# RWKV layers of a four-layer sequence on Trainium2: outer mixes and decays moved beside a unit's spreading, one inner mix interleaved with the decay product, gates held back

## The chip, the core and the metric

The program runs on one core of one Trainium2 chip. The time is the device time of one execution in microseconds; before the change it is 3452.1 us, the median of three runs (3450.18 to 3452.9). One further execution was recorded by the hardware profiler.

Names of engines in the profile: PE is the matrix engine (PEld its weight loads), DVE the vector engine, ACT the scalar engine, POOL the general one, SP the one that mostly issues DMAs (SPq and ACTq are the queues from which DMAs are issued). Each engine runs its own instructions in program order and waits for others through semaphores.

## The reference, cut to what matters

Four layers follow each other: a grouped cross attention, an RWKV block, a second cross attention with a feed-forward part, and another RWKV block. The input x is 16 x 100 x 512. Only the two RWKV blocks (layers 1 and 3) are touched. One of them computes, per batch:

```python
xa = _ln(x, ln1_w, ln1_b)
sx = concat([state[:, 1:2] - xa[:, :1], xa[:, :-1] - xa[:, 1:]], axis=1)
xxx = tanh((xa + sx * maa_x) @ maa_w1).reshape(b, l, 5, 32)
xxx = einsum('blfd,fde->blfe', xxx, maa_w2)
xm = xa[:, :, None] + sx[:, :, None] * (maa_stack + xxx)
xk, xw, xv, xr, xg = (xm[:, :, j] for j in range(5))
w = exp(-exp(time_decay + tanh(xw @ td_w1) @ td_w2))
r, k, v = xr @ Wr.T, xk @ Wk.T, xv @ Wv.T
g = silu(xg @ Wg.T)
# per head, over time: out_t = r_t (u * k_t v_t^T + s);  s = k_t v_t^T + w_t * s
og = groupnorm(out) * gn_w + gn_b
x1 = x + og * g @ Wo.T
# then the channel mix: xk2, xr2 from a second layer norm,
return x1 + sigmoid(xr2 @ Wfr.T) * (square(relu(xk2 @ Wfk.T)) @ Wfv.T)
```

All data are float32. There are 32 heads of 16 channels. The product with `maa_w1` has 160 columns, 32 for each of the five mixes f = 0 (k), 1 (w), 2 (v), 3 (r), 4 (g).

## The kernel before, in words

The 16 batches are taken in NG = 4 groups of G = 4, so a group has T = 400 tokens. The 512 channels lie as NC = 4 chunks of 128 partitions. A product of a chunk with a weight is 128 x 128 by 400 columns, and a full projection of one output chunk is a chain of four such products into one PSUM bank.

**Units.** The recurrence is cut into 128 units per layer: 4 groups x 4 chunks x 8. In one unit u (the loop at the end of `rwkv`):

- `spread(u + 1)`: PE copies rows of v to the 128 partitions, two products of 32 rows each (`vb<-vc,sel`). Even units use rows 0 to 63 of the array, odd ones rows 64 to 127. ACT then puts the starting state in column 0.
- `product(u)` and `scan(u)` on DVE: multiply by k, then two scans over time with w; POOL multiplies the result by r (`a<-a,rr`). There are two `vbs` buffers, so the spreading of unit u + 1 waits for the scan of unit u - 1.
- every second unit `gather`: four products of 32 columns each into the bank `acc` (`acc<-a,gat`); once per chunk (8 units) `bonus` (a product with `ones`, fed by POOL's `rk`, and four with `center`) and `norm` (a product with `mean`, started by `slots.begin()`).

**Pieces.** All other PE work of the layer is cut into pieces, listed by `piece(us, fn, slot, tag)` and taken in order while a budget `due` lasts: each unit adds 2.37 us (u below 29), 2.75, or 3.5 in the last 32 units, minus shares for the gather, bonus and norm, and each piece takes off its listed price. A `chain` is two pieces of two products each. `projections(g, base)` lists a group's pieces and is called at u = 32(g - 1) - 10, so a group's projections run during the units of the group before it; group 0's run ahead of unit 0. In order they are: statistics (DVE), `root` (POOL, gives `rstd` and `shift`) and `normed` (ACT, `xn_a`), priced 0; `turned`: transposes per chunk, ACT writes `ext`, POOL `sx`, then ACT `sm` and POOL `xm`; `inner(0, 128)` and `inner(128, 160)`: the first product with `maa_w1`, whose tanh gives `z0` (mixes 0 to 3) and the upper part of `tz` (mix 4); `mixed(fs, c)`: the second product of a mix for chunk c, 32 rows by 128 columns (mix f lies in rows 32f to 32f + 31; mix 4 in rows 64 to 95), read by DVE (`tm`) one unit later and finished on POOL (`xj`); `plain`: k, v, r; `decay_in`: 128 rows by 64 columns, tanh into the lower part of `tz`; `decay`: 64 rows (0 to 63) by 128 columns, two exponentials on ACT; `gate`: chains with Wg, a tanh on ACT and a product on DVE (`g2`). k, v, r, w and g go to DRAM from ACT's queue and come back through SP's queue.

In the last 32 units the pieces are the channel mix of groups 0 to 2 (`channel_stream`); the output product Wo of a group comes 7 units after its last unit, and group 3's Wo and channel mix follow the last unit.

**Banks.** Three PSUM banks (`Slots`) go round among all pieces. Taking a bank makes the reading of its former content be issued first (`readers`), otherwise `read_later` issues it at `slots.begin()` of the next unit, which stands ahead of the scan on DVE. Instructions of PE, DVE, ACT and POOL keep the program's order; DMAs on SP are placed by the framework.

**Lines.** Nearly all operations are recorded under the lines of helpers (L82 for a product, L85 for a transpose, L77 for DVE, ACT and POOL), so groups are told apart by their tiles: `mm<-z,maa_w2a` is an outer mix 0 to 3, `mm<-tz,td_maa_w` with 32 rows mix 4 and with 64 rows a decay, `mm<-xm,maa_w` the inner mix, `mm<-xj,td_w` the first decay product, `mm<-xj,l_Wg` a gate. The profile counts each float32 product as two MATMUL instructions.

## Time and profile before

| | |
|---|---|
| runs | 3450.18, 3452.1, 3452.9 us |
| the profiled execution | 3447.39 us, span of its instructions 3445.6 us, granted PE clock 0.942 |
| busy over the span | PE 3121.5 us (91%), DVE 1753.5 (51%), POOL 1373.2 (40%), ACT 977.3 (28%) |
| scans, `a<-wr,vb` on DVE | 512 x 971 ns |
| products by k, `vb<-vb,kr` on DVE | 256 x 977 ns |
| products by r, `a<-a,rr` on POOL | 256 x 1880 ns |
| spreadings, `vb<-vc,sel` on PE | 1024 instructions, 252.7 us busy |
| outer mixes 0 to 3 on PE | 256 instructions, 73.6 us busy |
| mix 4 and decays on PE | 128 instructions, 56.5 us busy |
| inner mixes on PE | 128 instructions, 67.4 us busy |

The first unit of layer 1 starts at 845.8 us (its spreading), the last at 1468.6; those of layer 3 at 2733.7 and 3352.6. A row of the windows gives a stretch of the span and the busy time of every engine in it. A row of the timeline gives the start, the time until the last end, engine, line, operation, tiles written and read, and in brackets how long the engine was idle and what ended that. Products overlap in the array: the time between two starts says more than the duration of one, and a product that waits inside the array for its data counts as busy.

### The profile page before, as it was taken

The numbers are of one execution on the slowest core, as the hardware profiler recorded it, in microseconds if no ns is written. First come the engines' busy times: TensorE is split into PE (matmuls) and PEld (weight loads), VectorE is DVE, ScalarE is ACT, GpSimd is POOL, SyncE is SP. The second block draws the span as 40 slices with busy tenths as digits, with TensorE's granted clock in tenths as the row PEclk, the third lists the DMA queues.
The fourth block names the chain that finished last, engine by engine and source line by source line (L and its number), as shares of the span: only waits on it lengthen the run. The fifth ranks groups of instructions, "written<-read, shape, count | busy, mean of one in ns | idle before, by whom it ended". The sixth has DMA issues, their size and how long they took to land. (4 is left out here: it accounts for less than half of the span.)

```text
span 3445.6 us, 47937 instructions
## 1 busy us (share of the span) xinstructions
PE 3121.5 (91%) x18371; PEld 1422.0 (41%) x18371; DVE 1753.5 (51%) x3570; ACT 977.3 (28%) x1715; POOL 1373.2 (40%) x1036
## 2 busy tenths in 40 slices
PE   6989898868999989988999999879998899998997
PEld 3434443334333333334455555445553433333333
DVE  4777777732877766523333333320001287766661
ACT  1333233222233333321323222211111233423332
POOL 0444444443775765521212111220002377676551
PEclk8999999979999989999999999989998999998998
DMA  5010100013335353222000000010011343535321
GB/s 173 22 31 22 31 22 34 1 32 115 113 108 150 109 173 108 77 72 64 28 19 20 19 20 31 26 64 10 10 58 34 111 129 102 150 116 174 91 70 50
DMA packets 171374, 240.18 MB, mean 70 GB/s; under 512 B 27678, under 2 KB 139358, under 8 KB 171146
## 3 DMA queue, kind: packets, MB, share of 16 engines
q1 hardware_dynamic: 148106, 204.35, 19.9%
q10 hardware_dynamic: 23040, 32.78, 2.7%
q8 instruction: 144, 2.36, 0.3%
q14 instruction: 84, 0.69, 0.1%
HBM read 174.25 MB, written 36.04 MB: 61 GB/s over the span
## 5 line engine op out<-in xcount | busy, mean ns | idle before, releaser
L77 POOL TENSOR_TENSOR a<-a,rr 128x800 f32<-128x800 f32 x256 | 480.9, 1880 | 331.0 <-DVE a L77 212.0
L77 DVE TENSOR_TENSOR_SCAN a<-wr,vb 128x400 f32<-128x400 f32 x512 | 475.9, 971 | 20.7 <-PE acc L82 9.1
L77 DVE TENSOR_TENSOR vb<-vb,kr 128x792 f32<-128x792 f32 x256 | 250.1, 977 | 184.7 <-ACT vb L77 184.5
L77 DVE CUSTOM_DVE_ANT_0 junk<-l_sc,mask 100x361 f32<-100x361 f32 x512 | 272.9, 533 | 87.1 <-PE l_sc L82 70.5
L82 PE MATMUL vb<-vc,sel 32*128 32x396 f32 x1024 | 252.7, 565 | 3.3 <-DVE a L77 3.3
L77 DVE TENSOR_TENSOR pt<-l_sc,maskT 121x400 f32<-121x400 f32 x384 | 193.4, 566 | 89.6 <-PE l_sc L82 88.8
L77 ACT ACTIVATE pt<-pt 121x1600 f32<-121x1600 f32 x96 | 147.6, 1538 | 282.4 <-DVE pt L77 280.8
L1490 DVE CUSTOM_DVE_ANT_0 junk<-l2a_sc,mask 100x361 f32<-100x361 f32 x256 | 136.9, 535 | 173.0 <-PE l2a_sc L82 155.8
L1526 POOL TENSOR_TENSOR pa<-pt,pt 121x1600 f32<-121x1600 f32 x16 | 57.1, 3569 | 362.3 <-ACT pt L1521 362.3
L77 POOL TENSOR_TENSOR xj<-tm,ext 128x400 f32<-128x400 f32 x160 | 150.6, 961 | 110.9 <-DVE tm L77 110.1
L77 DVE SCALAR_TENSOR_TENSOR tm<-mm,vec,sx 128x400 f32<-128x400 f32 x160 | 95.7, 628 | 185.5 <-PE mm L82 149.4
L82 PE MATMUL k<-ct,l_k_w 128*128 128x361 f32 x512 | 173.3, 482 | 14.4 <-DMA ct<-in_ctxT 14.4
L1707 DVE TENSOR_TENSOR x<-pb,x 100x512 f32<-100x512 f32 x16 | 12.2, 760 | 335.4 <-DMA pb<-po 330.3
L77 POOL TENSOR_TENSOR pa<-pt,pt 121x1600 f32<-121x1600 f32 x32 | 114.7, 3583 | 165.0 <-ACT pt L77 165.0
L63 PE MATMUL h<-yTb,l_fc 128*128 128x400 f32 x512 | 174.5, 503 | 6.3 <-ACT yTb L229 6.3
L82 PE MATMUL v<-l_v_w,ct 128*121 128x512 f32 x384 | 175.5, 601 | 0.0
L63 PE MATMUL p<-l_proj,h 128*128 128x512 f32 x384 | 165.5, 592 | 0.0
L77 ACT COPY vb<-s0r 128x8 f32<-128x8 f32 x256 | 42.9, 168 | 407.8 <-PE vb L82 320.4
L82 PE MATMUL l_sc<-kz,qz 32*100 32x361 f32 x1024 | 116.7, 526 | 42.9 <-DVE pt L77 22.0
L82 PEld LDWEIGHTS vb<-vc,sel 32*128 32x128 f32 x1024 | 81.9, 191 | 154.0 <-issue 113.5
L63 PEld LDWEIGHTS h<-yTb,l_fc 128*128 128x128 f32 x512 | 97.7, 192 | 81.1 <-ACT yTb L229 8.3
L77 POOL TENSOR_TENSOR pa<-pa,pt 119x1600 f32<-119x1600 f32 x32 | 114.4, 3576 | 41.1 <-ACT pt L77 40.9
(258 smaller groups left out, 5174.2 us busy)
## 6 DMA issues: line engine op xcount, KB each, us to landing
kr<-dk SPq DMA_DIRECT2D x256, 100.0 KB
wr<-dw SPq DMA_DIRECT2D x256, 100.0 KB
rr<-dr SPq DMA_DIRECT2D x256, 100.0 KB
ct<-in_ctxT SPq DMA_DIRECT2D x32, 722.0 KB
dk<-k ACTq DMA_DIRECT2D x32, 200.0 KB
kc<-dk SPq DMA_DIRECT2D x32, 200.0 KB
dw<-wd ACTq DMA_DIRECT2D x32, 200.0 KB
dv<-v ACTq DMA_DIRECT2D x32, 200.0 KB
```

Source lines behind the costliest of these rows:

```text
L63: nc.tensor.matmul(out=ps, lhsT=lhs(c), rhs=rhs(c), start=(c == 0), stop=(c == n - 1))
L77: return lambda *args, **kw: tc.keep_in_program_order(op(*args, **kw))
L82: pin(nc.tensor.matmul(**kw))
L1490: nc.vector.tensor_tensor_reduce(out=junk, in0=ss[r][:L, :S2], in1=t["mask"], scale=-1.0, scalar=FLT_MAX, op0=ALU.add, op1=ALU.min, accum_ ...
L1526: nc.gpsimd.tensor_tensor(t["pa"], t["pt"][0], pt, ALU.add)
L1707: nc.vector.tensor_tensor(x, pb[:, i, :], x, ALU.add)
```

## The change

- `Slots` remembers the bank of an open chain (`held`) and passes it over when a bank is asked for.
- `piece` takes two more values, `half` and `ok`. A new function `beside(u)` is called once per unit, after `slots.begin()` and before `scan(u)`: it takes the first piece whose `half` is u % 2 (row half 0 for mixes 0 and 1 and for the decays, half 1 for mixes 2, 3 and for mix 4), if that piece's `ok` allows it, and charges 0.12 us to the budget. PE gets it right after the spreading of unit u + 1, which uses the other half of the rows, or after the chunk's `mean` product where one is issued at `slots.begin()`.
- `inner` now makes only the first 128 columns. The last 32 (mix 4) are made in `decay_in`: for each chunk one 64-column product with `td_w1` into partitions 0 to 63 of a bank and one 32-column product with `maa_w1` into partitions 64 to 95, and one tanh reads both.
- The order of a group's pieces is new: inner mix, mixes 0 and 1, `decay_in`, all of k, mixes 2 and 3, decays, all of v, all of r, mix 4.
- The gates are not listed with their group but held in `held`: the next group's list takes them in among its first pieces (two half chains ahead of the inner mix, four behind it, two behind `decay_in`), and the last group's stand in the channel stream after its first transposes.
- The budget per unit is 1.9 (from 2.37) for u below 29 and 2.4 (from 2.75) up to the last 32 units.

```diff
         def bank(self):
             t = next(self.turns)
+            if t is self.held:
+                t = next(self.turns)
             self.readers.pop(id(t), lambda: None)()
             return t
...
+            def beside(u):
+                half = u % 2
+                p = next((p for p in pieces if p[4] == half and p[1] <= u), None)
+                if p is None or not p[5]():
+                    return 0.0
+                pieces.remove(p)
+                p[2]()
+                return 0.12
...
+                older, taken = list(pieces), set()
+                behind = [(p[0], base - 1 if g > 1 or i > 3 else -1000, *p[2:]) for i, p in enumerate(held)]
...
                 def decay_in():
+                    bank = []
+                    def half(i):
+                        if i == 0:
+                            for fn in soon + mixes[1]:
+                                fn()
+                            slots.held = slots.bank()
+                            bank.append(slots.held)
+                            begun.append(second)
+                        else:
+                            begun.clear()
+                            slots.held = None
+                        ps = bank[0]
+                        for c in (2 * i, 2 * i + 1):
+                            mm(
+                                out=ps[:64, :T], lhsT=td1[:, c, :], rhs=xj[1][:, c, :],
+                                start=(c == 0), stop=(c == NC - 1),
+                            )
+                            mm(
+                                out=ps[64:96, :T], lhsT=w1[:, c, 128:160], rhs=st["xm"][:, c, :],
+                                start=(c == 0), stop=(c == NC - 1),
+                            )
+                        if i:
+                            scalar.activation(st["tz"], ps[:96, :T], AF.Tanh)
+                            taken.add("tz")
...
-                inner(0, 128)
-                mix((0, 1), 0)
-                mix((0, 1), 1)
-                inner(128, 160)
-                mix((0, 1), 2)
-                mix((0, 1), 3)
+                free = {
+                    (0, 1): lambda: "z0" in taken and not any(p in pieces for p in older),
+                    (2, 3): lambda: "tz" in taken and not any(p in pieces for p in older + behind),
+                    (4,): lambda: "tz" in taken and all(("k", c) in taken for c in range(NC)) and ((2, 3), 0) in taken,
+                }
+                pieces.extend(behind[:2])
+                inner()
+                pieces.extend(behind[2:6])
+                for c in range(NC):
+                    mix((0, 1), c)
+                decay_in()
+                pieces.extend(behind[6:])
                 for c in range(NC):
                     plain(0, "Wk", "k", c)
+                for c in range(NC):
                     mix((2, 3), c)
-                decay_in()
...
+                for co in range(NC):
+                    piece(0.67, lambda co=co: decay(co), late, None, 0, lambda: "tz" in taken)
...
-                for co in range(NC):
-                    gate(co)
+                held[:] = written(lambda: [gate(co) for co in range(NC)])
...
                 for k in ("stats", "normed", "turned"):
                     got += parts[0][k]
+                got += [(p[0], slot - 1, *p[2:]) for p in held]
+                held.clear()
...
                 slots.begin()
+                aside = beside(u) if unit and u + 1 < UNITS else 0.0
                 if unit:
                     scan(u)
...
-                due = min(due, 0.0) + (2.37 if 0 <= u < 29 else 2.75 if u < UNITS - 32 else 3.5 if u < UNITS else 3.9)
+                due = min(due, 0.0) + (1.9 if 0 <= u < 29 else 2.4 if u < UNITS - 32 else 3.5 if u < UNITS else 3.9)
+                due -= aside
```

## The prediction, made before the changed kernel ran

> **What bounds the kernel now.** I read the four 32-unit stretches of the first RWKV layer as a table of windows, then TensorE's timeline inside them, then the other queues at the places where TensorE stood. The windows (start:end, length, then busy us and instructions of PE, PEld, DVE, ACT, POOL, then clock and DMA):
> ```profile
> 845.80:978.70 132.90, 126.09 (x503) 48.95 (x502) 103.26 (x130) 43.51 (x97) 92.38 (x76) 0.93 0.35 107
> 978.70:1128.00 149.30, 143.54 (x578) 55.73 (x576) 109.14 (x137) 49.85 (x105) 99.88 (x82) 0.94 0.43 127
> 1128.00:1293.40 165.40, 151.78 (x587) 57.88 (x586) 111.08 (x139) 55.26 (x113) 113.30 (x97) 0.90 0.48 144
> 1293.40:1468.50 175.10, 162.79 (x713) 64.53 (x712) 107.09 (x133) 64.06 (x127) 95.41 (x77) 0.93 0.31 89
> ```
> PE is the fullest engine in each. Layer 3 repeats them (132.7, 147.5, 166.8 and 172 us), so everything below counts twice. The scan work of DVE is a floor of about 105 us per stretch, POOL's 92 to 113.
>
> What a piece costs on PE, from its timeline:
> ```profile
> 955.32 0.94 PE L82 MATMUL vb<-vc,sel 32*128 32x396 f32 x4
> 956.18 0.88 PE L82 MATMUL acc<-a,gat 128*32 128x400 f32 x8
> 956.99 1.61 PE L82 MATMUL mm<-xj,l_Wg 128*128 128x400 f32 x4
> 958.53 0.60 PE L82 MATMUL vb<-vc,sel 32*128 32x396 f32 x2
> ...
> 1070.16 0.60 PE L82 MATMUL mm<-tz,td_maa_w 32*128 32x400 f32 x1
> 1070.16 0.60 PE L82 MATMUL vb<-vc,sel 32*128 32x396 f32 x2
> 1070.60 0.49 PE L82 MATMUL mm<-tz,td_maa_w 32*128 32x400 f32 x1
> 1070.60 0.50 PE L82 MATMUL vb<-vc,sel 32*128 32x396 f32 x2
> 1071.03 0.88 PE L82 MATMUL acc<-a,gat 128*32 128x400 f32 x8
> ...
> 1203.71 1.61 PE L82 MATMUL mm<-tz,td_maa_w 64*128 64x400 f32 x4
> 1205.24 0.93 PE L82 MATMUL vb<-vc,sel 32*128 32x396 f32 x4
> ```
> Every product is two passes. By starts: a spreading 0.87, a gather 0.81, half a chain (two products) 1.54. Passes of a chain start 0.335 apart, so a product is 0.67 and each change of tile form (rows x columns of the array) costs 1.54 - 2 x 0.67 = 0.20; a lone product is 0.87. The second block is an outer mix beside a spreading, both 32x128, in other rows: together 0.87, so the mix is free. The third is two decays (64x128, rows 0 to 63) ahead of a spreading in rows 64 to 127: free rows too, yet it starts only after the decays' 1.53, 0.43 after their last pass. Same tile form overlaps; another form waits.
>
> Adding these prices over the order of the products gives 117.2, 134.7, 137.4 and 155.1 us for the stretches. Where PE runs through they agree with the clock: units 40 to 47 add to 35.8 and took 35.5, 48 to 55 add to 32.5 and took 32.3. So PE waits 15.7, 14.6, 28.0 and 20.0 us in the stretches (the page counts a product waiting in the array as busy). The waits sit at group starts:
> ```profile
> 823.03 10.91 PE L82 MATMUL mm<-xj,l_Wg 128*128 128x400 f32 x32
> 841.31 0.43 PE L85 MATMUL mm<-ident,xn_a 100*128 100x100 f32 x1 [7.37 <-ACT xn_a L77]
> ...
> 981.42 1.70 PE L82 MATMUL mm<-rk,ones 128*128 128x400 f32 x2 [1.75 <-POOL rk L77]
> 985.85 5.21 PE L82 MATMUL mm<-xm,maa_w 128*128 128x400 f32 x8 [1.23 <-POOL xm L77]
> 990.99 0.93 PE L82 MATMUL vb<-vc,sel 32*128 32x396 f32 x4
> ```
> Ahead of unit 0 PE is out of work after the last gate, because DVE takes group 1's statistics only after that gate's product; POOL's `shift` and ACT's `xn_a` follow. At unit 32 the inner mix takes 5.2 instead of 2.9 us, waiting on POOL's `xm`.
>
> **The change part by part (first layer; all on PE unless said).**
>
> *Mixes beside a spreading.* Of 36 mix pieces in units 0 to 127, 9 already fall next to a spreading in other rows; in the new order 22 do. 13 x 0.87 = -11.3. (Where a chunk's `mean` product is emitted in between, they do not.)
>
> *Decays beside a spreading.* 64x128 after 32x128: no overlap by the 1205.24 row. 12 decays that mostly went in pairs (1.54, so 0.77 each) go alone at 0.87: +1.2. They are charged 0.12 in the budget, so the units carrying them get more work than planned.
>
> *Second inner mix alternating with the first decay product.* No row has a 64-column next to a 32-column product in free columns. Bounds: if columns overlap, eight products take 4 x 0.67 + 0.20 = 2.9 against 6.2 for the four halves before (-3.3 per group); if each alternation waits as rows of unequal height do, 8 x 0.87 = 7.0 (+0.8). I take the second, the nearest row: 3 groups, +2.4. In group 0, ahead of unit 0, the product follows POOL's `xj` (eight at 0.96) anyway, so it is about level there.
>
> [...]
>
> *Budget and pieces cut differently.* A few more half chains and changes of form: +1.2. Together -6.5 on PE. By place, the new order adds to 109.1, 133.0, 132.8 and 153.7 (-15.8) in the stretches, and 9.2 us of channel products that used to lie inside now follow unit 127.
>
> *After unit 127.* Those 9.2 us precede the Wo products; before, PE waited there 4.2 us on POOL's last `gc`, and about 3 of that is covered: +6.
>
> *Ahead of unit 0.* Group 0's gates now wait for group 1's list, so DVE's program has two of the four statistics (0.85 each) ahead of the second gate's product and two right behind it, not all four behind the last. In the times of before: that product ends at 829.8, the last statistics at 831.5, POOL's `shift` (1.7) at 833.2; ACT's first `xn_a` ends at 834.0, when the gates end as well, and the transposes start there instead of at 841.3: -7. The last gate's tanh now stands behind the four `xn_a` on ACT, ahead of `kc` and `ext` (0.5). The stretch of PE from the first mixes to the last gate gets about 2 shorter, since the decay product comes while PE would wait for POOL's `xj`; half of it I count: -8 in all. What is late next is `ext`, `sx`, `xm` for the first inner mix, as before.
>
> *Group starts.* Unit 32: transposes are split over units 31 and 32, POOL's order becomes `a`, `rk`, two `sx`, two `xm`, `a`, two `sx`, two `xm`: from the end of scan 30, 1.9 + 1.0 + 1.9 + 1.9 + 1.9 + 1.7 + 1.9 = 12.2 to the last `xm`; PE has 8.1 us of work there, so it still stands about 5; the held gates then cover `z0`. Three pairs of mixes in one unit through three banks wait about 2 for DVE's reads. Waits 14.6 -> about 9 in the second stretch, PE -1.7: -7. The first stretch: PE -8.1, waits 15.7 -> about 11 (its first inner mix still waits 5 for `xm`; DVE, now near the bound at 3.3 us per unit while mixes run, takes the rest): -13. Third and fourth: PE -6.0; group 3's start -5, as the second's; at the channel stream (units 94 to 96, 18 us of wait) gates stand where key products stood, but `rk` now lies behind eight `xk`/`xr` on POOL (7.7) and the bonus product waits for it, so only about 2 is won: -13.
>
> SP and POOL queues: the `gc` loads keep places behind the gates' stores; no load of `kr`, `wr`, `rr` stands behind one whose store comes later. POOL issues no DMA. ACT loses one tanh per group; cost nothing at 44 of 133 us busy.
>
> **Sum.** -8 - 13 - 7 - 13 + 6 = -35 per layer; 2 go off for small bank waits of the 12 decays (about 0.15 each, estimated): -33, and -66 for both. The profiled execution took 3447.4 us (span 3445.6); the three runs have a median of 3452.1, so 4.7 more. 3447.4 - 66 + 4.7 = 3386.
>
> **Rivals.**
> 1. *Columns overlap.* For: eight passes of a gather in four column groups take 0.81. Against: those are one form. Six scanned groups gain 4.1 each: -24, 3362.
> 2. *The waits stay.* For: POOL chains end the waits, and filler does not shorten them. Against: PE order ahead of unit 0 is plainly freed. PE -15.8 + 6 per layer, nothing else: 3452 - 20 = 3432.
> 3. *Slower: mixes and decays right after a spreading wait for their bank.* A bank is free only when DVE has read it, and that read can stand behind a pair of scans (1.86 us). Some 12 pieces per group, 6 groups, all ahead of gather and chains in PE's order: 72 x 1.86 = +134 at most, 3520. It decides from 66/72 = 0.92 us per piece. Against: reads are placed ahead of the scan at the next unit's start, and at 3.3 us per unit they end 1.5 us before the decay.
>
> **How the numbers follow.** Forecast 0.52, rival 1 0.15, rival 2 0.13, rival 3 0.16, no measurable change 0.04. Within 0.2% (7 us) is about what a measurement of this kernel cannot tell from no change. Faster 0.80, same 0.04, slower 0.16. The range: from rival 1 with stretch waits 8 per layer smaller (3346) to rival 2 with every decay waiting 0.6 for its bank, 7 per layer (3446); it leaves out most of rival 3 and what lies past these ends.
>
> **What would show it.** Right: transposes ahead of unit 0 within 3 us of the last gate; mixes with the start of a spreading; decay rows starting 0.43 after a spreading's last pass; alternating decay and inner products 0.87 apart (rival 1: starts within 0.05); first stretch near 120. Wrong: PE idle before mix or decay released by DVE `tm` at many units, or unit 0 as late as before.

## The result, and the profile after

The changed kernel takes 3427.7 us (median of seven runs, 3422.3 to 3442.8); the kernel before took 3451.0 in the seven runs beside it. The ratio is 0.9939 with a 95% interval of 0.9923 to 0.9955: faster by 21 us by the ratio (23 by the medians), a third of the 66 that were forecast. The profiled execution took 3425.9 us with a span of 3424.0 (before 3447.4 and 3445.6).

The four stretches of layer 1 after the change, as a table of windows (start:end, length, then busy us and instructions of PE, PEld, DVE, ACT, POOL, then granted PE clock, DMA share, GB/s):

```profile
846.07:970.75 124.68, 119.60 (x481) 43.87 (x480) 103.22 (x127) 41.27 (x92) 92.61 (x76) 0.94 0.37 110
970.75:1112.62 141.87, 135.43 (x582) 51.44 (x581) 108.88 (x138) 50.45 (x104) 98.93 (x81) 0.98 0.45 136
1112.62:1269.00 156.38, 141.59 (x582) 54.02 (x582) 109.49 (x136) 53.91 (x109) 105.23 (x89) 0.91 0.46 141
1269.00:1452.61 183.61, 163.29 (x714) 64.96 (x713) 109.29 (x138) 64.16 (x129) 102.38 (x85) 0.91 0.33 97
```

Against 133, 149, 165 and 175 us before: three stretches gain 8.3, 7.4 and 8.9 us and the last loses 8.4. Layer 3 has 124.7, 141.9, 155.5 and 181.8 (before 132.7, 147.5, 166.8, 171.8). From the first outer mix to unit 0, where 8 us were to be won, it is 80.1 us in both kernels and both layers. Behind the start of the last unit layer 3 takes 3.6 us more (96.7, from 93.0); layer 1's interval from there to layer 3's first mix, with the untouched layer 2 in it, takes 5.8 us more.

The edits themselves do what the diff says. PE's timeline of the changed kernel:

```profile
869.49 0.89 PE L82 MATMUL mm<-xj,td_w 128*64 128x400 f32 x2
870.31 0.86 PE L82 MATMUL mm<-xm,maa_w 128*32 128x400 f32 x2
871.10 0.60 PE L82 MATMUL vb<-vc,sel 32*128 32x396 f32 x2
871.11 0.60 PE L82 MATMUL mm<-z,maa_w2a 32*128 32x400 f32 x2
...
874.33 0.94 PE L82 MATMUL vb<-vc,sel 32*128 32x396 f32 x4
875.20 0.94 PE L82 MATMUL mm<-tz,td_maa_w 64*128 64x400 f32 x2
```

A mix starts 0.01 us after a spreading and costs nothing. A decay starts 0.87 after it, so it does not overlap. The decay product and the inner mix in other columns start 0.8 us apart, where products of one form start 0.67 apart: these, 64 and 32 columns wide, don't overlap either.

What differs from the forecast is seen ahead of unit 0. Group 0 of layer 1 in the changed kernel, PE's timeline:

```profile
791.02 4.93 PE L82 MATMUL mm<-z,maa_w2a 32*128 32x400 f32 x16
795.89 5.39 PE L82 MATMUL mm<-tz,td_maa_w 64*128 64x400 f32 x8
801.36 13.52 PE L82 MATMUL mm<-xj,l_Wv 128*128 128x400 f32 x32
814.72 10.91 PE L82 MATMUL mm<-xj,l_Wr 128*128 128x400 f32 x32
...
828.44 11.65 PE L82 MATMUL mm<-xj,l_Wg 128*128 128x400 f32 x32
840.50 0.30 PE L85 MATMUL mm<-ident,xn_a 100*128 100x100 f32 x1 [0.41 <-ACT xn_a L77]
```

The wait ahead of the transposes is 0.41 us, from 7.37, as forecast. But the gates start at 828.4 and not at 823.0. The value chains took 13.5 us where the same 32 passes of the r chains took 10.9, and the four decays 5.4 where their price is 2.7. The same place in windows of 3.41 us shows why (length, PE busy first, the clock third from the end):

```profile
785.98:789.39 3.41, 3.41 (x12) 1.95 (x11) 0.00 (x0) 0.76 (x2) 0.00 (x0) 1.00 0.77 232
789.39:792.80 3.41, 3.29 (x13) 1.28 (x11) 0.73 (x2) 0.49 (x1) 0.02 (x1) 1.00 0.79 239
792.80:796.22 3.42, 3.42 (x11) 1.71 (x12) 3.30 (x6) 0.00 (x0) 3.42 (x4) 1.00 0.44 129
796.22:799.63 3.41, 3.41 (x6) 1.67 (x5) 0.67 (x2) 1.13 (x2) 3.41 (x5) 0.50 0.00 0
799.63:803.04 3.41, 3.32 (x6) 1.38 (x5) 0.00 (x0) 1.90 (x4) 0.69 (x5) 0.50 0.27 93
803.04:806.46 3.42, 3.42 (x6) 1.77 (x6) 0.00 (x0) 1.48 (x3) 0.00 (x0) 0.50 0.86 263
806.46:809.87 3.41, 3.41 (x11) 1.94 (x11) 0.00 (x0) 0.81 (x2) 0.00 (x0) 1.00 0.26 93
```

From 796.2 to 806.5 PE runs at half clock: 10.2 us, of which 5.1 are lost. It was shown busy through the whole window before that (792.80 to 796.22); what that window held were mixes of 32 rows and the first decay.

Counted from the first mix, the gates begin 5.1 us later than before and take 0.7 longer, the wait behind them is 7.0 shorter, and from the first transpose to unit 0 it takes 1.1 longer: together 0.

### The profile page after: what moved, and what is told of

Same layout as the page of the kernel before. It is cut to its first block, busy times and chain, and to the rows that moved or that the text cites. A ratio compares the mean times of both kernels' runs of the same rounds, so it can differ in the third digit from the quotient of the medians.

```text
span 3424.0 us, 47912 instructions
## 1 busy us (share of the span) xinstructions
PE 3105.1 (91%) x18371; PEld 1412.6 (41%) x18371; DVE 1755.0 (51%) x3570; ACT 975.3 (28%) x1707; POOL 1369.9 (40%) x1036
## 5 line engine op out<-in xcount | busy, mean ns | idle before, releaser
L77 POOL TENSOR_TENSOR pa<-pt,pt 121x1600 f32<-121x1600 f32 x32 | 114.8, 3586 | 165.3 <-ACT pt L77 165.3
L82 PEld LDWEIGHTS vb<-vc,sel 32*128 32x128 f32 x1024 | 81.0, 187 | 156.4 <-issue 99.5
L63 PEld LDWEIGHTS h<-yTb,l_fc 128*128 128x128 f32 x512 | 98.2, 192 | 83.2 <-ACT yTb L231 10.0
```

The lines of the kernel that those rows point to most:

```text
L63: nc.tensor.matmul(out=ps, lhsT=lhs(c), rhs=rhs(c), start=(c == 0), stop=(c == n - 1))
L77: return lambda *args, **kw: tc.keep_in_program_order(op(*args, **kw))
L82: pin(nc.tensor.matmul(**kw))
```

## An account with the clock in it

The prediction compared the sum of product prices with the time of a stretch and called the difference waits. All the time at half clock was in that difference, though the clock column of the windows it quoted said 0.93, 0.94, 0.90 and 0.93. One of its own lines shows it. The inner mix at 985.85, 5.2 us for eight passes, was read as waiting inside the array for POOL's `xm`. PE did stand 1.23 us for `xm` ahead of it, but its passes then start 0.67 us apart until 990.0, and the clock there is half:

```profile
980.20:990.40 10.20, 7.75 (x17) 3.18 (x18) 4.33 (x6) 2.51 (x4) 10.12 (x13) 0.50 0.74 204
```

Nor does the trace of before show, elsewhere in the two RWKV layers, a product that waits inside the array and counts as busy, as was assumed ahead of the run: no pass there lasts longer than 0.72 us at full clock. So the account has to have three parts. In the traces of before and of the changed kernel the clock is either 1.0 or 0.5 and changes only on a grid of 3.41 us (90 and 94 spells, each a multiple of it but the last, which the end of the trace cuts). The time lost to it is half of the time for which products ran inside half-clock spells (a pass taken as 0.335 us at full clock, 0.67 at half); what is then left over the prices is waiting. The prices are sums over the order of the products and the waits a remainder, so their differences between two kernels are surer than the single values. Layer 1, before and after, in us:

| units | time | prices | at half clock | lost by it | waits |
|---|---|---|---|---|---|
| 0-31 | 133.0, 124.7 | 117.2, 109.1 | 18.4, 15.0 | 8.2, 6.2 | 7.6, 9.4 |
| 32-63 | 149.3, 141.9 | 134.7, 133.0 | 18.1, 6.8 | 7.0, 2.9 | 7.5, 6.0 |
| 64-95 | 165.3, 156.4 | 137.4, 132.8 | 32.2, 27.3 | 9.8, 8.2 | 18.1, 15.3 |
| 96-126 | 175.2, 183.6 | 155.1, 153.7 | 24.8, 34.1 | 9.7, 11.1 | 10.5, 18.8 |

Both layers together: prices -31.6, which is what the new order was reckoned to give, clock loss -11.2, waits +11.6, in sum -31.2. With +9.4 behind the last units, 0 ahead of unit 0 and +0.3 before the first mix of layer 1 that is the 21.5 us between the profiled executions, up to rounding.

PE's idle time before (length less busy time in the prediction's four rows: 6.8, 5.8, 13.6 and 12.3 us) lies nearer to the waits of this account than to the 15.7, 14.6, 28.0 and 20.0 of the prediction.

The waits after the change sit mostly at the channel stream. In layer 1 unit 94 takes 8.5 us more than its prices and unit 96 8.8, units 113 and 114 together 11.5, units 124 and 125 10.2 (time lost at half clock is in these figures). Here is the pair at units 94 and 96, first PE, then POOL, of the changed kernel:

```profile
1258.86 0.43 PE L85 MATMUL mm<-ident,xn_1b 100*128 100x100 f32 x1 [7.38 <-ACT xn_1b L77]
...
1276.78 1.70 PE L82 MATMUL mm<-rk,ones 128*128 128x400 f32 x2 [6.87 <-POOL rk L77]
```

```profile
1272.02 0.97 POOL L77 TENSOR_TENSOR xk_1b<-mxk_1b,ext_1b 128x400 f32<-128x400 f32 x1
1272.93 0.98 POOL L77 TENSOR_TENSOR xr_1b<-mxr_1b,ext_1b 128x400 f32<-128x400 f32 x1
1273.85 1.89 POOL L77 TENSOR_TENSOR a<-a,rr 128x800 f32<-128x800 f32 x1
1275.68 1.05 POOL L77 TENSOR_TENSOR rk<-rc,kc 128x400 f32<-128x400 f32 x1
```

The transposes wait for normalised rows whose statistics come only after unit 93's scans on DVE; then `rk` waits behind eight `xk`/`xr` of 0.97 us. Both times that PE stands here the clock falls as well: 13.7 us at half clock from 1254 on, 6.8 from 1274.

## Experiments

The theory that came out of the traces (theory C below): PE's clock falls to half after a 3.41 us window in which few rows of the array were streamed, whether PE stood still or was busy with narrow products. The rivals: it falls only when PE stands; or it plays no part, and the time is set by chains through DVE, POOL and ACT.

**Group 0 in its old order.**

```diff
+                if g == 0:
+                    first_group(inner, mix, plain, decay)   # the order of before
+                    held[:] = written(lambda: [gate(co) for co in range(NC)])
+                    return
```

> The changed kernel, with group 0 of each layer (the work ahead of unit 0) in the order of the kernel before: the second inner mix as its own chain, key products between mixes 2 and 3, the decay product as a chain, decays in pairs between value products; gates still held back. Theory A (the freed wait ahead of unit 0 was spent by group 0's new order on PE, which made the last gate end 5.5 us later): unit 0 starts 5 to 7 us earlier in each layer, the time is 10 to 14 us below the changed kernel, about 3415. Rival B (unit 0 is held by the statistics, shift and normalisation on DVE, POOL and ACT whatever PE does): unit 0 starts within 1 us of the changed kernel's, the time is the same, about 3428.

3432.5 us, ratio to before 0.9951 (0.9933 to 0.9968): not to be told from the changed kernel. Yet from the first mix to unit 0 it took 75.9 us, not 80.1, in both layers, and time at half clock there went from 19.1 to 8.0: theory A had the place right, and the clock is what did it. The next 32 units took most of the gain back. Two windows of this run, from about the first mix to unit 0, and units 0 to 31:

```profile
769.00:844.81 75.81, 71.98 (x209) 33.74 (x209) 17.33 (x32) 18.34 (x34) 21.97 (x31) 0.95 0.40 122
844.81:972.87 128.06, 122.34 (x480) 44.66 (x479) 103.33 (x127) 41.36 (x92) 92.53 (x76) 0.91 0.36 107
```

Units 0 to 31 have the very order of the changed kernel: prices 109.1 in both, waits 9.1 and 9.4. Only the clock differs, 0.91 to 0.94: 22.8 us at half clock and not 15.0, 9.9 lost and not 6.2, which with the 0.3 less of waits is the whole difference of 3.4. The windows do not start with the work: counted from unit 0, the half-clock spell in units 1 to 3 lies at 12.5 to 22.8 us in this run and at 15.0 to 18.4 in the changed kernel.

The same old order of group 0 is in six of the later runs, and there the time from first mix to unit 0 goes with the clock: 72.5 to 72.6 us where 1 to 3 us of it are at half clock, 73.9 with 3.5, 74.2 to 74.3 with 7, 75.9 to 76.0 with 8. One of the former, from the run with the chain apart in groups 1 to 3 below:

```profile
773.73:846.26 72.53, 69.05 (x210) 32.91 (x210) 17.35 (x32) 18.36 (x34) 21.99 (x31) 0.98 0.43 128
```

That is 7.5 us less than before (where 12.4 us of this part ran at half clock), nearly the 8 that were forecast.

**The alternation taken apart.**

```diff
-                        for c in (2 * i, 2 * i + 1):
-                            mm(out=ps[:64, :T], ...td1...)
-                            mm(out=ps[64:96, :T], ...w1...)
+                        for c in range(NC):
+                            # half 1: the four td1 products; half 0: the four w1 products
```

> The changed kernel, with the alternation of the decay product and the second inner mix taken apart: the first half issues the four 32-column products, the second the four 64-column products; all else stays. Theory A (neighbours of another column width wait, 0.80 per product against 0.67 within a form): each group's eight products take about 5.8 instead of 6.4 us, six groups beside units and two ahead of them: 3 to 5 us below the changed kernel, about 3424. Rival B (columns of another width overlap in part, so that alternation gains): 2 to 10 us above the changed kernel.

3428.1 us, 0.9945 (0.9925 to 0.9966). PE's prices fall by 1.1 us per group, as theory A says, and the time does not move: the four stretches take 124.7, 142.7, 155.1 and 181.8 us. In the first two stretches waits and clock take the 1.1 back (0.8 and 0.3 us, 0.2 and 1.7). The alternation costs a little on PE and nothing that shows in the time, though these few runs (3425.8 to 3431.9) could hardly tell the 3 to 5 us of theory A.

**Gates at home.**

```diff
-                held[:] = written(lambda: [gate(co) for co in range(NC)])
+                for co in range(NC):
+                    gate(co)
```

> The changed kernel, with a group's gates in its own list again (not held back for the next group's). Theory A (holding them is what took the 7 us wait ahead of unit 0 away, and what covers the later groups' starts): PE waits 6 to 8 us ahead of the transposes before unit 0 in each layer again, and the inner mix of groups 1 to 3 waits longer: 15 to 30 us above the changed kernel, 3443 to 3458. Rival B (the wait ahead of unit 0 was filled by nothing that counts, and gates only change places): within 5 us of the changed kernel. Rival C (held gates push the channel streams' starts back): up to 10 us below it.

3433.1 us, 0.9956 (0.9943 to 0.9969): 5 us above the changed kernel by the medians, with intervals that overlap: less than theory A asked for, about what rival B allowed. The wait ahead of the transposes is back (5.78 us, `xn_a`), and from first mix to unit 0 it takes 84.4 and 86.3 us. Holding the gates back is worth these 4 to 6 us per layer at that place. In the stretches behind, prices are 6.0 us per layer higher without it, from work that otherwise follows unit 127, and waits 4 to 6 lower.

**No step beside the spreading.**

```diff
-                aside = beside(u) if unit and u + 1 < UNITS else 0.0
+                aside = 0.0
-                due = min(due, 0.0) + (1.9 if 0 <= u < 29 else 2.4 if u < UNITS - 32 ...)
+                due = min(due, 0.0) + (2.37 if 0 <= u < 29 else 2.75 if u < UNITS - 32 ...)
```

> The changed kernel, without the step that takes mixes and decays beside a spreading: they come by the budget again, in the list's order, and the budget is that of the kernel before. Theory A (a mix beside a spreading saves PE 0.87 us and PE is the bound wherever mixes run): 13 of them per layer, 11 us, 15 to 23 us in both layers above the changed kernel, 3443 to 3450. Rival B (the stretches are set by the waits on POOL's chains, and freed PE time only lengthens waits): within 5 us of the changed kernel.

3480.9 us, 1.010 (1.0079 to 1.012): 53 above the changed kernel and 30 above the one before, far beyond theory A. By the account of both layers' stretches, against the changed kernel, prices rise by 10 us, waits by 5.5, and the loss to the clock by 37. Units 0 to 31, and PE's timeline inside them:

```profile
852.33:997.83 145.50, 135.80 (x492) 51.69 (x491) 105.48 (x130) 43.83 (x95) 94.08 (x77) 0.84 0.33 98
```

```profile
966.26 0.93 PE L82 MATMUL vb<-vc,sel 32*128 32x396 f32 x4 [0.91 <-DVE a L77]
970.32 1.69 PE L82 MATMUL vb<-vc,sel 32*128 32x396 f32 x4 [3.12 <-DVE a L77]
971.94 1.56 PE L82 MATMUL acc<-a,gat 128*32 128x400 f32 x8
```

Taken from the new list by budget, the mixes come three and four in a row, the decays three in a row, and pieces run out before the end. Then DVE's scans are what PE waits for, and its clock is half (a gather's eight passes take 1.56 us, where they took 0.88 at full clock). So most of what the step gives is not 0.87 us per mix: it strews the 32-row pieces among wide ones.

**A strip of products at the end.** It measures the clock by itself, with products whose results nobody reads.

```diff
+            if last:
+                for rows, cols, n in ((128, 128, 30), (32, 128, 30), (64, 128, 20), (128, 128, 15),
+                                      (64, 128, 30), (128, 128, 10), (128, 32, 30), (32, 128, 12), (128, 32, 30)):
+                    for i in range(n):
+                        mm(out=acc[:cols, :T], lhsT=w2a[:rows, :cols], rhs=w2a[:rows, :T], start=True, stop=True)
```

> The changed kernel, followed at its very end by a strip of products that nobody reads, back to back on TensorE without a wait, 400 columns each (two passes): 30 of 128 rows x 128 columns, 30 of 32x128, 20 of 64x128, 15 of 128x128, 30 of 64x128, 10 of 128x128, 30 of 128x32, 12 of 32x128, 30 of 128x32. It adds work and changes no result; only the strip is read. Theory C (the clock follows the rows that are streamed in each 3.4 us window, as the windows of the earlier traces suggest: full to half when rows x time falls to 0.40 or less of the window, half to full from about 0.73): the 32x128 products start at 0.67 us apart and go to 1.34 within 3 to 7 us; the 64x128 after them stay at 1.34; 128x128 bring full clock back within 3 to 7 us; 64x128 after full clock stay at 0.67; 128x32 stay at 0.67; 32x128 then fall to 1.34 and 128x32 come back to 0.67. Rival B (the clock falls only when TensorE stands still): 0.67 apart all through, clock 1.0. Rival D (it follows the share of the array, rows x columns): as theory C, but 128x32 falls to half as 32x128 does.

The one execution took 3603.5 us, and only the strip is read. Windows inside it, in its order: 32x128 early and late, 64x128 after them, 128x128, 64x128 again, 128x32, 32x128 and 128x32:

```profile
3446.00:3449.00 3.00, 3.00 (x10) 1.67 (x9) 0.00 (x0) 0.00 (x0) 0.00 (x0) 1.00 0.00 0
3455.00:3479.00 24.00, 24.00 (x37) 11.97 (x37) 0.00 (x0) 0.00 (x0) 0.00 (x0) 0.50 0.00 1
3481.00:3506.00 25.00, 25.00 (x39) 12.64 (x38) 0.00 (x0) 0.00 (x0) 0.00 (x0) 0.50 0.00 0
3512.00:3519.00 7.00, 7.00 (x22) 3.99 (x21) 0.00 (x0) 0.00 (x0) 0.00 (x0) 1.00 0.00 0
3520.00:3539.00 19.00, 19.00 (x58) 10.64 (x57) 0.00 (x0) 0.00 (x0) 0.00 (x0) 1.00 0.00 1
3547.00:3566.00 19.00, 19.00 (x58) 6.20 (x57) 0.00 (x0) 0.00 (x0) 0.00 (x0) 1.00 0.00 0
3573.00:3577.00 4.00, 4.00 (x8) 1.88 (x6) 0.00 (x0) 0.00 (x0) 0.00 (x0) 0.50 0.00 0
3584.00:3600.00 16.00, 16.00 (x49) 5.28 (x48) 0.00 (x0) 0.00 (x0) 0.00 (x0) 1.00 0.00 1
```

PE never stands inside the strip, and the clock goes as theory C has it at every step: 32-row products bring it to half within 6 us (starts 0.67, then 1.33 apart), 64-row products leave it where it is, at 0.50 after narrow ones (3481 to 3506) and at 1.00 after wide ones (3520 to 3539), and products of 128 rows bring it back (1.00 from 3512 to 3519), even with 32 columns (1.00 from 3584 to 3600). Rival B (standing still) and rival D (share of the array) fall. So in the strip the clock went by the rows that were streamed, not by the time that PE was busy and not by the columns.

Does that hold inside the kernel? For each 3.41 us window around the two layers I added up, over all passes, the share of the 128 rows times the pass's time (passes side by side in other rows added, in the same rows counted once), as a share of the window. In the trace of before all 22 windows after which the clock fell have at most about 0.37 and all 338 at full clock that stayed there at least about 0.37. In five other traces (the changed kernel, group 0's old order, no step beside, and two kernels below) the highest that fell is 0.45 and the lowest that stayed 0.37; back to full clock it took, in these traces, between 0.64 and 0.81. The strip's 64-row products, with a share of 0.5, lie between the two bounds. The share of the window in which any product ran does not separate them: one with 0.88 fell, one with 0.39 stayed.

**The second inner mix as its own chain between the outer mixes**, in groups 1 to 3, and group 0 as above.

```diff
-                for c in range(NC):
-                    mix((0, 1), c)
-                decay_in()
+                mix((0, 1), 0)
+                mix((0, 1), 1)
+                chain(... w1[:, c, 128:160] ...)      # 128 rows by 32 columns
+                mix((0, 1), 2)
+                mix((0, 1), 3)
+                chain(... td1[:, c, :] ...)
```

> The changed kernel, with group 0 as in the run with group 0's old order and, in groups 1 to 3, the second inner mix as its own chain of four between the outer mixes, the decay product as its own chain behind them, so that 128-row products stand between the 32-row mixes; mixes and decays still beside spreadings, gates still held back. Theory C (the clock falls where a 3.4 us window holds hardly anything but 32-row products; an account of the changed kernel by product prices, half-clock time and waits leaves 6 us of clock loss in the first stretch of 32 units, 3 in the second, 8 in the third, 11 in the fourth): half-clock time in the first three stretches falls from 49 to about 30 us per layer, unit 0 comes 4 us sooner after the first mix than in the changed kernel, product prices fall by 1 us per group: 10 to 20 us below the changed kernel, 3408 to 3418. Rival (the windows run free, and a fall avoided at one place comes at another; half-clock time stays within 5 us per layer): 0 to 8 us below, 3420 to 3428.

3432.6 us, 0.9947 (0.9931 to 0.9962): no gain over the changed kernel, on the rival's side and above even its range. Up to unit 0 it took 72.5 us (80.1), units 0 to 31 took 120.1 and 121.9 (124.7), but units 64 to 95 167.8 and 160.5 (156.4 and 155.5). In layer 1's third stretch half-clock time rose from 27 to 44 us and waits from 15 to 19, around group 3's mixes and its later decay product. In layer 1 the half-clock time of the first three stretches rose to 59 us from 49, where theory C had 30. What one place gave, another took.

**The start of the channel stream.** Three edits, each alone on the changed kernel:

```diff
-                for k in ("stats", "normed", "turned"):            # earlier statistics
-                    got += parts[0][k]
+                for k, ahead in (("stats", 6), ("normed", 2)):
+                    got += [(0.0, slot - ahead, *p[2:]) for p in parts[0][k]]
+                got += parts[0]["turned"]
...
-                    soon.append(slots.defer(1, mix))               # mixes later
+                    soon.append(slots.defer(1 + c // 2, mix))
...
-                    got += p["first"] + q["stats"] + p["second"] + q["normed"]      # transposes earlier
-                    got += p["third"] + q["turned"] + p["fourth"]
+                    got += p["first"] + q["stats"] + p["second"][:2] + q["normed"] + p["second"][2:4]
+                    got += q["turned"] + p["second"][4:] + p["third"] + p["fourth"]
```

> The changed kernel, with the statistics and the normalisation of the first channel part put out six and two units earlier, ahead of the transposes in unit 94. Theory A (TensorE stands at unit 94 because the transposes wait for normalised rows, which wait for statistics put out only just before): the 8.5 us of unit 94 above its product prices fall to 2 to 4 us, units 88 to 96 get 5 to 7 us shorter per layer, 10 to 14 us in all. Rival B (the statistics wait for the last output rows of group 0 to 2, whenever they are put out): DVE stands earlier instead, 0 or slower. Rival E (the next wait, of unit 96 for the bonus product's operand, grows by what unit 94 gives): 0 to 3 us.

> The changed kernel, with the channel part's eight mixes on POOL put out one to two units later for the last two chunks, so that the bonus product's operand of unit 96 stands behind four of them and not eight. Theory A (unit 96 waits 8.8 us because that operand stands behind eight mixes of 0.97 us on POOL): four fewer, 3.9 us less in unit 96, of which the key products behind take 1 to 2 back: 2 to 4 us per layer, 4 to 8 in all. Rival B (the transposes' late start sets unit 96 and not POOL's order): within 1 us per layer.

> The changed kernel, with the normalisation and the transposes of the next channel part put ahead of the second half of the rows of the part before (two gate rows and two value rows). Theory A (TensorE stands at units 113 and 125 because a part's key products wait for POOL's eight mixes, which come straight after its transposes): units 112 to 127 lose 8 to 14 of their 21 us above product prices, and 10 us of half-clock time: 8 to 14 us less per layer, 16 to 28 in all. Rival (the transposes then wait for the normalised rows in front of the gate and value rows, and TensorE stands there): 0, or up to 10 us more.

One execution each: 3413.4, 3422.0 and 3421.3 us. The changed kernel's seven runs lie between 3422.3 and 3442.8, so the last two times alone show no gain; the places do. With earlier statistics unit 94's 8.5 us are gone (theory A), and in layer 1 4 of them come back at unit 96, 12.8 instead of 8.8 (theory E in part). With later mixes unit 96 of layer 1 falls from 8.8 to 2.6, more than said, and units 94 to 96 take 26.6 and 29.4 us in the two layers, from 32.2 and 33.0. Earlier transposes only move the place where PE stands: unit 112 now takes 11.7 us above its prices, because `rk` waits there behind the same eight mixes, and units 112 to 126 take 96.1 and 92.9 us, from 98.2 and 96.4. That is nearest to the rival, with another wait than it named.

**Edits together.** The first two of them; then with group 0's old order and the earlier transposes; then with the chain apart in groups 1 to 3:

> The changed kernel with the two edits that acted on the start of the channel stream together: statistics and normalisation of the first part earlier, and POOL's last mixes one to two units later. One alone gave 3413 and the other 3422 in one execution each, but with the first the wait of unit 96 grew from 8.8 to 12.8 us, and the second takes just that wait. If the waits add up: 8 us per layer from unit 94 and 6 to 9 from unit 96, 28 to 34 us below the changed kernel, 3394 to 3400. If the clock's windows take part of it back: 3400 to 3412. If they don't add up: 3413.

> The kernel of the two channel edits, with group 0 in its old order (128-row products between the 32-row mixes) and the next channel part's transposes earlier. Group 0 gives 4 us per layer ahead of unit 0, of which the clock's windows in units 0 to 31 took 3 back in the run of that edit alone; the transposes 4 to 7 per layer if they act: 3382 to 3400. Rival (nothing adds): as the two channel edits alone.

> As the run before it, and in groups 1 to 3 the second inner mix as a chain of its own between the outer mixes. In the run with that edit and group 0's the first stretch took 120 to 122 instead of 125 us, but the third 161 to 168 instead of 156. If the third stretch's loss was the clock at the channel stream's start, which the channel edits shorten: 3 to 8 us below the run before it, 3376 to 3395. If it was the later decay product of group 2: 3 to 8 us above it.

3416.1 us, ratio to before 0.9901 (0.9871 to 0.9930); 3381.5, 0.9805 (0.9774 to 0.9837); 3389.8, 0.9837 (0.9799 to 0.9874). The first pair did not add up: unit 96 of layer 1 still takes 11.2 us above its prices. The second came out at the low end of its forecast: units 96 to 126 take 171 and 167 us in place of 184 and 181. The transposes, which alone only moved the place of the wait, pay once POOL's last mixes come later: unit 112 stands 6.3 us above its prices and not 11.7. The third lost in the third stretch what it won in the first, as in the run of that edit with group 0: 161 and 162 us, 37.5 of them at half clock. Its interval overlaps the second's.

**All mixes behind `rk`, and the chain apart by group.**

```diff
-                    soon.append(slots.defer(1 + c // 2, mix))
+                    soon.append(slots.defer(2 + c // 2, mix))
...
+                if g == 1:      # then g < 3: the chain between the mixes; other groups as in the changed kernel
```

> As the kernel of the two channel edits, group 0's old order and the earlier transposes, but all eight mixes of the channel part on POOL are put out another unit later, so that the bonus product's operand of unit 96 comes ahead of all of them and not behind four. Theory A (the 9.8 us that unit 96 still takes above its prices are those mixes: 1271.3 to 1278.8 on POOL holds four mixes, a scan's product and then that operand): unit 96 falls to 5 to 6 us above its prices, 4 us per layer and up to 2 of clock: 6 to 12 us below that kernel's 3381, 3369 to 3376. Rival (the key products of unit 98 then wait for the mixes by as much): 3379 to 3384.

> As the run before it, and the second inner mix as its own chain between the outer mixes in group 1 alone (units 0 to 31). Theory C (128-row products between 32-row ones keep the clock up; the place where that pays is the first stretch: 8 us of half clock there against 17 to 23): the first stretch takes 120 instead of 126 to 128 us in both layers, 8 to 14 us below the run before it, 3357 to 3367. Rival (the later decay product gives it back, or a fall of the clock comes elsewhere): within 4 us of it.

> As the run before it, and that chain apart in group 2 as well (units 32 to 63), not in group 3. In the second stretch it took 143.5 us where the alternation took 142 to 146: within 4 us of the run before it. It also tells whether group 3 alone made the third stretch 161 us in the kernel with all groups apart: here the third stretch should take 144 to 149.

3370.5 us, 0.9759 (0.9726 to 0.9792); 3355.4, 0.9717 (0.9682 to 0.9751); 3363.8, 0.9744 (0.9715 to 0.9774). The POOL order is what unit 96 waited for. POOL and PE with all mixes later:

```profile
1254.09 1.87 POOL L77 TENSOR_TENSOR a<-a,rr 128x800 f32<-128x800 f32 x1
1255.93 1.02 POOL L77 TENSOR_TENSOR rk<-rc,kc 128x400 f32<-128x400 f32 x1
1256.96 0.97 POOL L77 TENSOR_TENSOR xk_1b<-mxk_1b,ext_1b 128x400 f32<-128x400 f32 x1
```

```profile
1257.00 1.30 PE L82 MATMUL mm<-rk,ones 128*128 128x400 f32 x2 [1.58 <-POOL rk L77]
```

The same row of the kernel without this edit:

```profile
1278.91 1.70 PE L82 MATMUL mm<-rk,ones 128*128 128x400 f32 x2 [8.37 <-POOL rk L77]
```

The wait is 1.58 us, from 8.37, and unit 96 of layer 1 stands 3.2 above its prices, from 9.8 (layer 3: 6.5, from 10.2). Units 94 to 96 take 19.4 and 19.2 us, from 22.9 and 23.0. With the chain apart in group 1 alone the first stretch takes 121.9 and 122.8 us (126.4 and 125.8 without), 15 us less in the medians of the whole, with intervals that overlap; the two profiled executions, 3361.4 and 3360.2, differ by 1.2 only, since in these other places took back what the first stretch gave. The third stretch stays at 146 to 148, and at 147.5 with the chain apart in group 2 as well: the loss there belonged to group 3's chain. Apart in group 2 as well it is 8 us slower by the medians, more than the 4 that were allowed, though the intervals overlap: the second stretch takes 143.3 and 143.4 us, not 141.9 and 140.8. Layer 1's windows of the kernel with the chain apart in group 1:

```profile
843.36:965.24 121.88, 116.32 (x479) 42.99 (x479) 102.95 (x127) 41.98 (x93) 92.53 (x76) 0.95 0.38 113
965.24:1107.10 141.86, 135.42 (x581) 51.57 (x580) 108.87 (x138) 50.54 (x104) 98.93 (x81) 0.98 0.47 136
1107.10:1252.72 145.62, 136.85 (x581) 52.37 (x581) 108.95 (x136) 50.60 (x104) 101.64 (x85) 0.96 0.50 150
1252.72:1420.32 167.60, 155.87 (x713) 62.97 (x712) 110.99 (x138) 66.48 (x133) 106.25 (x89) 0.96 0.38 107
```

It computes the same products on PE as the changed kernel, 72 us faster by the medians; in the traces time at half clock fell from 392 to 294 us over the span, which is worth up to 49 us; the rest is shorter waits and slightly lower prices.

## Why the prediction was wrong, step by step

- *What a piece costs on PE*: right. The new order was reckoned 15.8 us per layer cheaper inside the stretches. In stretches that run through the sum meets the clock: units 48 to 55 add to 30.0 and took 29.7.
- *Second inner mix alternating with the first decay product*: right in kind. Starts are 0.8 us apart, 0.87 was taken, rival 1 (columns overlap) is out. The run without the alternation shows no cost in the time.
- *Ahead of unit 0*, -8: failed, it was 0.0. The wait of 7.37 us was freed as described (0.41). But the step priced group 0's new order at full clock, even as 2 us shorter; with all mixes 2 and 3 and all decays in a row, the clock fell for 10.2 us and the gates began 5.4 later (5.1 counted from the first mix). The transposes then took 1.1 longer to unit 0. What the prediction had named as a sign of being wrong, unit 0 as late as before, came true. Group 0's old order in the same kernel gives 4.2 and 4.0 us, and 7.5 where hardly any of it runs at half clock: the step's mechanism held and its clock did not.
- *Group starts*: the step had 15.7, 14.6, 28.0 and 20.0 us of waits per stretch and took some 17 of them off. About half of the first two was clock (8.2 and 7.0), the 5.2 us of unit 32's inner mix among it. Unit 32's stretch gave its -7 by luck: 4.1 of it came from the clock and 1.5 from waits, where 5.6 of waits were meant. The first gave -8.3 for -13: prices as said and 2.0 less lost to the clock, but waits rose by 1.8 where 5 were to go; no run shows why. The third and fourth gave -0.5 in layer 1 and -1.3 in layer 3 for -13: the "about 2" to be won at the channel stream turned into a loss, 19.2 us at units 94 to 96 where it was 18.2, and another 3 to 4 at the later parts, which stood at units 110 and 122 before and stand at 113 and 125 now. `rk` behind eight mixes was seen and priced; what that does at the later parts was not.
- *After unit 127*, +6: 3.6 in layer 3, where it can be read alone; up to 5.8 in layer 1.
- *Bank waits*, 2 per layer: the size by luck. No run shows 0.15 us per decay: all 24 decays behind a spreading start 0.42 us after its last pass, without idle time. But units 6, 8 and 10, with a pair of mixes beside the spreading, stand 0.7, 1.2 and 0.7 us above their prices.
- *The rivals*: the second (the waits stay, 3432) came nearest to 3427.7, and for its reason: waits that end on POOL's chains are not shortened by taking work off PE. That the sum fits so well is luck in part: less time lost to the clock (-11.2) and longer waits (+11.6) cancel. The third (slower by bank waits) needed 0.92 us for each of 72 pieces; the three units just named add to 2.6 us.

So two steps failed: group 0's new order was priced at full clock (-8 forecast, 0 measured), and of the term called waits far more was taken off than went. That term held two things that react differently: chains through other engines, which lighter PE work did not shorten (waits +11.6 us with prices 31.6 lower), and time at half clock, which went with the *order* of products (19.1 us ahead of unit 0 in the new order, 8.0 in the old).

## What to carry to other kernels

Before calling the gap between product prices and elapsed time "waits", take out half of the busy time at half clock: the clock column of the windows has it, and in layer 1 it was 34.7 of the 78.3 us that were called waits. Then look where products of few rows stand together. In group 0's new order the 32-row mixes and the first decay filled 3.41 us; 10.2 us at half clock followed, in which passes take 0.67 us each and not 0.335. In its old order, with 128-row products between them, 8.0 us ahead of unit 0 ran at half clock where it had been 19.1, and in some runs 1 to 3. Then look at every place, for what one place gained here another often lost. And where a chain through another engine ends a wait, look at that engine's order: with the last four of POOL's mixes put later, units 94 to 96 took 5.6 and 3.6 us less in the two layers, and with all of them behind one operand another 3.5 and 3.8, with no work taken off PE.

## What the runs showed of the hardware that was not expected

In the strip PE's clock followed the rows that were streamed. 32-row products brought a busy PE from 1.00 to 0.50 within 6 us, 64-row products ran at 0.50 behind them and at 1.00 behind 128-row ones, and with 128 rows by 32 columns the clock was back at 1.00 as with 128 by 128. A pause is not needed for a fall: PE was busy for all of the strip's 176 us, and its clock fell to half twice. In the traces of before and of the changed kernel the clock is 1.0 or 0.5, and its 90 and 94 spells are multiples of 3.41 us, but for the last, which the end cuts.

That grid is not tied to the work: counted from unit 0, the half-clock spell in units 1 to 3 began at 12.5 us with group 0's old order and at 15.0 in the changed kernel, with the same order of products in these units. So the same instructions take different times. The part up to the first mix of layer 1, which no edit here touches, took between 763.6 and 774.0 us in the profiled executions, with 82 to 109 us at half clock: the shortest with the least, the longest with the most. Group 0's old order gained 4.2 us ahead of unit 0 of layer 1 and lost 3.4 in the 32 units behind, with the same code there; only the account by place showed both.
